# First PReLU in one ScalarE and one VectorE pass, softmax's nine exponentials in SBUF with its product on GpSimd, and new places in the order

## Chip, cores and metric

The kernel runs on one core of one Trainium2 chip. The core has five engines that run side by side, each through its own queue in order: TensorE (PE in the profile; its weight loads are PEld), VectorE (DVE), ScalarE (ACT), GpSimd (POOL) and SyncE (SP), whose queue issues all DMAs here. The metric is device time in microseconds, as the median of several runs. Before the change it is 1863.83 us, the median of 3 runs between 1862.01 and 1864.88.

## What is computed

The input x is 16 images of 256 channels by 56 by 56, fp32. Two layers follow each other, both of the form x + f(group_norm(x)). In layer 0, f takes the sign of the normalised input, convolves it three times with binarised 3 by 3 weights (dilations 1, 3, 5; 4 groups of 64 channels), passes each result through a PReLU, adds the three and normalises over channels. In layer 1, f is an attention over the 3 by 3 neighbourhood of each pixel, with 8 heads of 8 channels.

```python
# layer 0
for i, d in enumerate((1, 3, 5)):
    y = conv(sign(gn(x) + bias), binarised(w[i]), dilation=d, groups=4)
    y = y + cb[i] - move1[i]
    y = where(y >= 0, y, alpha[i] * y) + move2[i]
    out = out + y
x = x + layer_norm_over_channels(out) * gamma + beta
# layer 1
q, k_in, v_in = split(gn(x) @ qkv_w.T + qkv_b)
k, v = branch(k_in) + rpb, branch(v_in)      # 9 neighbours and a learned depthwise part
attn = softmax((q * k).sum(channels of the head), over the 9 neighbours)
x = x + (attn * v).sum(9) @ proj_w.T + proj_b
```

## The kernel before

**Tiling.** Channels lie on partitions, 64 of a group twice: the upper and the lower half of the image sit on partitions 0 to 63 and 64 to 127. An image is done in two units (u = 0, 1), each of 2 x 7 rows in both halves: 784 elements per partition. A tile in PSUM is a pair of banks ([128, 2, 512]); there are four of these pairs, and every matrix product of the kernel goes through one of them.

**Stages of an image.** `signs` reads the image, gets its group statistics (L643) and writes the signs (L667). For each unit, `conv` runs for 4 groups and 3 dilations (24 convolutions an image): 36 matmuls (L716) into a pair, then the PReLU, then `channel_norm` (L799 to L863): sums over channels by matmul (L769), mean subtraction on VectorE (L827), scaling (L837), the residual sum on GpSimd (L850), and squares for the next group norm (L854). `fold` puts the second group norm into the q/k/v weights, `qkv` makes q, k and v (L906, evicted by ScalarE at L924). `scores` multiplies q with nine shifted k (L959, the query-key products), sums them per head by matmul (L980) and does the softmax; `attend` spreads the attention by matmul (L1044), multiplies with shifted v on VectorE (L1055), adds up on GpSimd (L1070), and projects (L1087, L1097).

**The PReLU.** With z the raw product, y = csc z + cbi, and PReLU(y) = alpha y + (1 - alpha) relu(y). So each convolution takes three passes: a linear one (asc z, where asc is csc alpha), a Relu by ScalarE in place in PSUM (L750), and VectorE's scalar_tensor_tensor that adds oalpha times the Relu (L755). The linear pass is ScalarE's for the first dilation (L735, which adds the constant mv2 of the channel too) and for the third (L742, into a tile `rl`, added to `ct` later by GpSimd at L761), and VectorE's for the second (L745).

**The softmax.** Eight of the nine scores of a head lie in a transposed PSUM tile, 104 heads-by-pixels of 8 per partition (832 elements); the ninth score is zero, so that the maximum is taken against zero. The exponentials of the eight go to SBUF (`et`, L1018), that of the ninth to unused columns of the PSUM tile (L1017). Then VectorE sums eight (L1019), adds the ninth (L1021), takes the reciprocal (L1025), multiplies (L1027) and transposes back (L1031).

**What sets the order.** The program is written as a list of operations with reads and writes. `ORDER` gives each operation a place: a number for each stage and position in it, plus `PERIOD` times the image. Stages of the first image carry the sign ^, those of the last $. `Plan.emit` takes, again and again, the operation with the lowest place whose predecessors have been emitted and whose buffers are free; this is the order in each engine's queue. A very low place thus means "as soon as it can". Operations written with `either` go to GpSimd, unless `ON_VECTOR` lists their position in the stage: then VectorE does them. Buffers: four PSUM pairs, eight `ct`, one `rl`, seven `p` (products), four `m`, one each of `et` and `at`.

```python
o = Op(PERIOD * self.image + ORDER[self.stage][k], emit, bufs)
...
todo = sorted(self.ops, key=lambda o: o.place)
while todo:
    o = next((o for o in todo if not o.wait and self.room(o)), None)
```

Of the kernel before, what the change touches and what calls it, by code (L numbers as in the profile page):

```python
# [8 lines left out]
F32 = mybir.dt.float32  # L9
# [5 lines left out]
P = 128  # L15
# [57 lines left out]
class Op:  # L73
    def __init__(self, place, emit, bufs):
# [6 lines left out]
PERIOD = 1231  # L81
ORDER = {
    "conv0": (
        -682, -410, -359, -2832, -303, -327, -265, -333, -280, -264, -245, -1566, -289, -213, -969, -970,
        -319, -128, -2067, -24, -3260, -58, -18, -16, -1028, -3936, 5, 17, 18, 101, 198, -321, 208, -3768,
        197, 207, 182, -601, -3937, 20, -15, -19, -199, 30, -146, 111, -2560, 21, -394, -20, -152, -3331,
    ),
    "conv0$": (
        -685, -409, -2692, -2836, -277, -2837, -419, -253, 194, -189, 109, -866, -1791, -207, -131, -440,
        -4781, -30, -3248, 99, -154, -250, -557, -386, -2111, -2366, 32, -462, -149, -2080, 175, -1794,  # L90
        -2185, -2439, 121, 140, -6017, -1732, -220, -9, -641, 100, -155, 112, -1493, 147, -1733, 191, 240,
        149, -865, -2379,
    ),
    "conv0^": (
        -2099, -6338, -223, -5746, -1337, -3215, -66, -5779, -1241, -202, -65, -5786, -1673, 42, -67, -667,
        -358, 124, 92, 358, -3217, 123, 231, 234, -3216, 565, 167, 400, 401, -1668, 228, 318, 504, -54, 229,
        -13, 515, -1726, -288, 227, 402, -115, -71, 40, -72, 517, -1182, 702, -116, -769, -2031, 119,
    ),
    "conv1": (
        160, -122, -123, 185, 199, -740, 209, -834, 265, -287, 150, -2506, -1087, 320, 171, 170, -823, 333,  # L100
        -2428, 361, -1220, 326, -175, 180, -1339, 356, 319, 255, 254, -2493, 355, -1340, 394, -1221, 714,
        746, 632, -113, -2040, 412, -162, -296, -1322, 470, -3611, 514, -1195, 925, -1683, -2369, 905, -1995,
    ),
    "conv1$": (
        56, -644, -645, -1492, 306, -11476, -498, -11477, 418, 239, 237, -3613, 188, 148, 146, 190, -1497,
        248, -878, 152, -867, 292, 151, -2181, -2390, -2392, 192, 98, 66, -864, 773, -432, 813, -1612, 662,
        456, 455, -1613, -818, 419, -28, -29, 44, 774, -431, 816, -434, 953, 968, 284, 678, -660,
    ),
    "conv1^": (
        666, 513, 523, -1198, 726, -697, -757, 826, 776, 581, 725, 830, 871, 682, 522, 601, -2033, 828, 824,  # L110
        695, 832, 829, 724, 578, 835, 715, 711, 612, 609, -2032, 865, 831, 878, 811, 949, 902, 901, 1044,
        1106, 38, 717, 718, 827, 869, 815, 890, -2027, 922, -1136, -964, 940, 959,
    ),
    "first^": (-3247,),
    "fold": (
        1404, -2035, -892, -2087, -3779, -4755, -952, -4221, -7223, -9967, -564, -942, -953, 1414, -949,
        -562, 1455, 407,
    ),
    "fold$": (
        1238, 1089, 753, 927, 1174, 593, 772, 1298, 934, 929, 595, 268, 1484, 297, 648, 1286, 559, -6518,  # L120
    ),
    "fold^": (
        1395, -941, -2847, -582, -784, 793, 792, -861, -863, -1498, -846, 1074, 1037, 696, 1424, -847, 1481,
        1444,
    ),
    "load0": (310,),
    "load0$": (539,),
    "load0^": (744,),
    "load1": (771,),
    "load1$": (614,),  # L130
    "load1^": (-117,),
    "mean0": (
        301, -2124, -1860, -2389, 172,
    ),
    "mean0$": (
        336, 87, 139, -232, -216,
    ),
    "mean0^": (
        785, 930, 214, -4431, 979,
    ),  # L140
    "mean1": (
        719, 911, 1038, -307, 787,
    ),
    "mean1$": (
        1195, -3235, -3236, -1711, 913,
    ),
    "mean1^": (
        1117, -960, 960, -337, -336,
    ),
    "norm0": (  # L150
        -732, -3656, -2175, -2045, -918, -715, -713, -2918, -1358, -2461, -2300, -2373, -2332,
    ),
    "norm0$": (
        -967, -5586, -5587, -2008, -2009, -2388, -1206, -2970, -3775, -3776, -5599, -1156, -4352,
    ),
    "prod0": (
        -1147, 777, -1035, 1488, 156, -3123, 155, -1057, -1219,
    ),
    "prod0$": (
        963, -2462, 449, -6519, 957, -392, -6024, 421, 1095,  # L160
    ),
    "prod0^": (
        -191, 8, -2267, -2417, -1351, -1352, 444, 443, 442,
    ),
    "prod1": (
        -3102, -1021, -550, -1863, 1762, 342, 1588, -2118, 615,
    ),
    "prod1$": (
        1043, 665, 309, 1102, 1281, 244, -3472, 1119, 1163,
    ),  # L170
    "prod1^": (
        1793, 1806, 1135, -4432, 1792, -1577, -69, 348, -1895,
    ),
    "proj0": (
        2327, 2254, 2286, 373, 2370, -2325, 2451, 1869, 1844,
    ),
    "proj0$": (
        4987, -693, 3217, 1049, 3039, -1400, 2317, -1399, -580,
    ),
    "proj0^": (  # L180
        2456, 2318, 2168, 956, 2213, 403, 2375, 410, 2115,
    ),
    "proj1": (
        2596, 566, 2594, 728, 2595, 31, 2582, 972, 1998,
    ),
    "proj1$": (
        45573, -572, 3218, -571, 45772, -1396, 44708, -1395, -465,
    ),
    "proj1^": (
        2523, 2564, 2522, -2377, 2607, 2566, 2508, -689, 1823,  # L190
    ),
    "qkv0": (
        1478, 1384, 1477, 1415, 1433, 1700, 1699, 387,
    ),
    "qkv0$": (
        1002, 836, 582, 610, -2708, 1260, 689, 1285,
    ),
    "qkv0^": (
        1490, 296, 1491, 1487, 1457, 1703, 685, 732,
    ),  # L200
    "qkv1": (
        1526, 1505, 1454, 1464, 1390, 1702, 1622, 712,
    ),
    "qkv1$": (
        1016, 619, 661, -3365, -1116, 1193, -1989, 1750,
    ),
    "qkv1^": (
        1514, 1090, 1467, 206, 1432, 1716, 551, 1624,
    ),
    "root0": (  # L210
        -323, -2507, -2508, 269, 181, -248, 245, -4518, -2509, 325,
    ),
    "root0$": (
        -1114, -4877, -4950, -2612, -1167, -77, -803, -5143, -195, 480,
    ),
    "root0^": (
        675, 216, 215, -4430, 892, 917, 881, -4445, 939, 1020,
    ),
    "root1": (
        230, -453, 161, -555, 768, 847, 743, 786, 916, 1244,  # L220
    ),
    "root1$": (
        554, -859, -860, -826, 842, 1105, 841, -3528, -3551, 1178,
    ),
    "root1^": (
        618, 129, 526, -1441, 1196, 1206, 1214, -1468, -1169, 1250,
    ),
    "scale0": (
        -2391, 308, 742, -657, 311, 552, -655, 352, -518, -1336, 995, 1083,
    ),  # L230
    "scale0$": (
        -3616, -530, 790, -3617, 1003, 241, -3628, -807, 585, -793, 528, 1088,
    ),
    "scale0^": (
        810, -2704, 1097, -2294, 932, 891, 945, 931, 741, 961, 1045, 820,
    ),
    "scale1": (
        886, -1324, 1341, -426, -1325, 1353, -427, -1862, 700, -848, -1134, 721,
    ),
    "scale1$": (  # L240
        -1608, -1879, 693, -2047, 933, 1050, -258, 94, 303, 639, -285, 299,
    ),
    "scale1^": (
        814, -2794, 1299, 658, 1033, 1223, -3076, -276, 1064, -3077, 1199, 1092,
    ),
    "second^": (
        -533, -33, -269, -5855, 451, 670, -3184, -3197, -1840, -2841,
    ),
    "sign": (
        -2935, -620, -1699, -748, -537, -497, -768, -351, -1710, -526, -1611, -387,  # L250
    ),
    "sign$": (
        -1806, -587, -690, -884, -1173, -1643, -1644, -406, -940, -917, -851, -827,
    ),
    "soft0": (
        9, -22, 1683, -1162, 1642, 1681, -558, 1274, 1482, -2383, -2384,
    ),
    "soft0$": (
        -161, -12, 709, -1106, -1117, 710, 1919, 1868, 1855, 1035, 1034,
    ),  # L260
    "soft0^": (
        1489, 802, 1647, -95, 1075, 1663, -111, -1410, -1369, 1319, 1463,
    ),
    "soft1": (
        441, 1789, 2048, 1788, 2054, 2034, 798, -383, 2119, 2137, 343,
    ),
    "soft1$": (
        -1857, -1858, 882, -1233, 2421, 2422, 1504, 1503, 1507, 1506, -1172,
    ),
    "soft1^": (  # L270
        677, -14, 2019, 809, 1715, 2038, 1866, -567, 1065, 1992, 1188,
    ),
    "start^": (
        -854, -3067, -598, -1842, -4706, -3059, -2934, -2823, -589, -736, -1682, -1681, -4293, -4179, -4129,
        -3138, -588, -388, -541, -5501, -586, -532, -5502, -4128, -3068, -3064, -449, -668, -3186, -3187,
        -3169, -3168, -3181, -1702, -226, -523, -539, -5503, -481, -1363, -3182, -3183, -3105, -3754, -447,
        -225, -756, -3172, -3590, -633, -3642, -3227, -200, 288, -344, -1586, -224, -1338, -3228, -3229,
        -3211, -3212, -201, -73, -3204, -3205, -5781, -76, -85, -3206, -62, -568,
    ),
    "stats": (  # L280
        -1755, -1273, -1265, -1692, -1019, -872, -1573, -996, -832, -1698, -871, -772,
    ),
    "stats$": (
        -1727, -1368, -1559, -1883, -1776, -1654, -1805, -1349, -1361, -1807, -1215, -1183,
    ),
    "term0": (
        1553, 1554, 1552, 1536, 1566, 1565, 1629, 1621, 1610, 1609,
    ),
    "term0$": (
        1054, 1130, 1129, 1128, 1073, 1072, 1071, 996, 1028, 1027,  # L290
    ),
    "term0^": (
        1555, 1548, 1546, 1568, 1576, 1577, 1627, 1408, 1407, 1409,
    ),
    "term1": (
        1721, 1729, 1733, 1732, 1767, 1768, 1778, 1619, 1781, 1620,
    ),
    "term1$": (
        1053, 1259, 1019, 1127, 1175, 1258, 1131, 1980, 1979, 1978,
    ),  # L300
    "term1^": (
        1728, 1717, 1358, 1679, 1357, 1918, 1389, 1349, 1580, 1317,
    ),
    "value0": (
        1731, 436, 1766, 437, 1761, 1776, 434, 1760, 1775, 286, 1585, 1779, 285, -552, 2037, -373, 222, 1937,
# [45 lines left out]
}  # L351

ON_VECTOR = {
    "conv0$": (12,),
    "conv1$": (25, 51),
    "prod0": (5,),
    "prod0$": (3, 4, 6, 8),
# [1061 lines left out]
```

## Time and profile before

| | |
|---|---|
| median of 3 runs | 1863.83 us |
| the profiled execution, its own time | 1872.31 us |
| its span, first to last instruction | 1870.5 us |
| PE busy | 1653.7 us (88%) |
| DVE busy | 1570.8 us (84%) |
| POOL busy | 1408.7 us (75%) |
| ACT busy | 1314.6 us (70%) |
| DMA, mean over the span | 116 GB/s |

A line of a group names the line of the kernel, the engine, the operation, the tile written and those read, shapes, how often, then the busy time in us and the mean of one in ns, and after the second bar the idle time of the engine just before these instructions with what ended it. In windows of the trace the columns are the stretch, its length, the busy time of PE, PEld, DVE, ACT and POOL with the number of instructions in brackets, the granted clock of PE, the share of DMA time and GB/s. In the middle of the run every image shows the same pattern again.

### The profile page before, as it was taken

To read this page: it belongs to the slowest core of one execution; us is meant where nothing else is said; L and a number is where in the kernel's file an instruction comes from. 1 tells how busy PE (TensorE), PEld (TensorE's weight loads), DVE (VectorE), ACT (ScalarE), POOL (GpSimd) and SP (SyncE) were. 2 spreads that over 40 slices of the span, in tenths; PEclk is the share of its full clock that TensorE was granted. 3 is DMA by queue.
4 is the path that set the end of the run, shared out by engine and by line. 5 is a ranking of instruction groups with operands and counts; after the bars stand their busy time and mean duration, and the time that the engine had idled before them with its cause. 6 is when DMAs were issued, how large, how long until landed. Compare 5 with 4: busy or idle time off the path is not lost.

```text
span 1870.5 us, 62125 instructions
## 1 busy us (share of the span) xinstructions
PE 1653.7 (88%) x27322; PEld 953.1 (51%) x27322; DVE 1570.8 (84%) x2217; ACT 1314.6 (70%) x1861; POOL 1408.7 (75%) x782
## 2 busy tenths in 40 slices
PE   4879899898999989898998989899898989989784
PEld 3546455454545545454554545455454545745341
DVE  8777979979797997979799797979979797997966
ACT  5988778677777867677786777778677787755320
POOL 2147769688686968868696886869688686967865
PEclk9799999999999999999999999999999999999897
DMA  7852655547475554647555464755547467223023
GB/s 178 200 113 43 143 123 122 126 93 155 96 158 111 124 126 92 149 102 155 115 120 124 96 151 101 156 113 124 123 94 150 101 147 172 62 69 74 11 61 69
DMA packets 102094, 217.03 MB, mean 116 GB/s; under 512 B 10816, under 2 KB 84672, under 8 KB 101568
## 3 DMA queue, kind: packets, MB, share of 16 engines
q1 hardware_dynamic: 101824, 213.06, 51.8%
q8 instruction: 214, 3.51, 0.8%
q14 instruction: 56, 0.46, 0.1%
HBM read 156.23 MB, written 51.38 MB: 111 GB/s over the span
## 4 chain that ended last, share of the span: by engine, by line
PE 53%; POOL 18%; DVE 16%; issue 6%; ACT 4%; DMA 1%; SPq 0%; POOLq 0%; DVEq 0%; ACTq 0%
PE banks L716 19%; POOL m L1070 13%; PE banks L906 12%; PE banks L980 9%; DVE m L1055 4%; PE banks L1044 3%; PE banks L769 3%; POOL xt L850 3%; PE banks L1087 2%; ACT banks L750 2%; DVE rl L755 2%; DVE ct L755 2%; POOL p L959 1%; POOL ct L761 1%; DVE m L1075 1%
## 5 line engine op out<-in xcount | busy, mean ns | idle before, releaser
L716 PE MATMUL banks<-sgn,wconv 64*64 64x392 bf16 x13824 | 656.7, 335 | 60.3 <-DVE m L1055 25.8
L716 PEld LDWEIGHTS <-wconv 64*64 64x64 bf16 x13824 | 442.8, 106 | 279.1 <-issue 94.7
L1070 POOL TENSOR_TENSOR m<-m 128x784 f32<-128x784 f32 x255 | 475.3, 1864 | 95.9 <-DVE m L1055 82.2
L959 POOL TENSOR_TENSOR p<-qt,kt 128x784 f32<-128x784 f32 x267 | 468.1, 1789 | 93.2 <-ACT qt L924 88.0
L750 ACT ACTIVATE banks<-banks,cbi,csc 128x784 f32<-128x784 f32 x384 | 370.3, 973 | 95.8 <-DVE ct L745 95.8
L761 POOL TENSOR_TENSOR ct<-ct,rl 128x784 f32<-128x784 f32 x125 | 233.3, 1866 | 252.7 <-DVE ct L755 147.8
L1044 PE MATMUL banks<-at,wv 64*64 64x392 f32 x2560 | 276.1, 510 | 56.5 <-DVE lv L821 22.6
L1055 DVE SCALAR_TENSOR_TENSOR m<-banks,vb,vt 128x784 f32<-128x784 f32 x288 | 289.6, 1022 | 25.4 <-POOL m L1070 17.6
L755 DVE SCALAR_TENSOR_TENSOR ct<-banks,oalpha,ct 128x784 f32<-128x784 f32 x256 | 258.1, 1026 | 17.1 <-ACT banks L750 16.4
L906 PE MATMUL banks<-xt,wf 64*64 64x392 f32 x3072 | 269.0, 491 | 0.0
L850 POOL TENSOR_TENSOR xt<-xt,ct 128x784 f32<-128x784 f32 x124 | 229.2, 1871 | 1.4 <-DVE ct L837 1.3
L980 PE MATMUL banks<-p,wk 64*64 64x392 f32 x2304 | 213.7, 489 | 2.8 <-POOL p L959 2.6
L742 ACT ACTIVATE rl<-banks,asc 128x784 f32<-128x784 f32 x128 | 116.7, 912 | 107.0 <-PE banks L716 103.0
L906 PEld LDWEIGHTS banks<-xt,wf 64*64 64x64 f32 x3072 | 131.2, 133 | 101.2 <-issue 68.3
L643 ACT ACTIVATE xh<-xh 128x1568 f32<-128x1568 f32 x120 | 180.6, 1507 | 0.7
L735 ACT ACTIVATE ct<-banks,mv,asc 128x784 f32<-128x784 f32 x128 | 128.5, 1004 | 73.0 <-PE banks L716 72.8
L755 DVE SCALAR_TENSOR_TENSOR rl<-banks,oalpha,rl 128x784 f32<-128x784 f32 x128 | 131.8, 1030 | 53.6 <-ACT banks L750 48.8
L1044 PEld LDWEIGHTS banks<-at,wv 64*64 64x64 f32 x2560 | 86.8, 134 | 176.3 <-issue 69.2
L745 DVE SCALAR_TENSOR_TENSOR ct<-banks,asc,ct 128x784 f32<-128x784 f32 x128 | 131.0, 1024 | 24.9 <-PE banks L716 21.3
L980 PEld LDWEIGHTS banks<-p,wk 64*64 64x64 f32 x2304 | 93.1, 133 | 93.4 <-issue 76.2
L854 ACT ACTIVATE ct<-xt,pr 128x784 f32<-128x784 f32 x128 | 120.2, 940 | 25.4 <-POOL xt L850 23.0
L1087 PE MATMUL banks<-m,wp 64*64 64x392 f32 x1024 | 106.4, 518 | 32.1 <-DVE m L1075 29.6
(115 smaller groups left out, 1870.6 us busy)
## 6 DMA issues: line engine op xcount, KB each, us to landing
xh<-in_x SPq DMA_DIRECT2D x248, 392.0 KB, 5.7
xt<-in_x SPq DMA_DIRECT2D x128, 392.0 KB, 9.2
out<-xt SPq DMA_DIRECT2D x128, 392.0 KB, 5.9
sgn<-sgn SPq DMA_DIRECT2D x128, 41.2 KB, 7.6
p<-in_w SPq DMA_DIRECT2D x12, 144.0 KB, 3.2
xt<-in_wk_parts SPq DMA_DIRECT2D x1, 1344.0 KB, 8.1
xt<-in_wv_parts SPq DMA_DIRECT2D x1, 1280.0 KB, 9.4
wq<-in_wqkv SPq DMA_DIRECT2D x1, 384.0 KB, 9.7
```

Of the source, the lines that this page charges most:

```text
L643: lambda func=func, col=col: nc.scalar.activation(inside(g) if b == 0 else image(xh), image(xh), func, accum_out=sums[:, col : col + 1]),
L716: nc.tensor.matmul(out=ps[q * GC : (q + 1) * GC, h, 0:SN], lhsT=wconv[h * GC : (h + 1) * GC, g, d, tap, :], rhs=sgn[g][h * GC : (h + 1) * ...
L750: lambda: nc.scalar.activation(n(), n(), AF.Relu, bias=cbi[:, g, s], scale=csc[:, g, s]),
L755: lambda: nc.vector.scalar_tensor_tensor(to.tile, n(), oalpha[:, g, s], to.tile, ALU.mult, ALU.add),
L761: lambda e: e.tensor_tensor(ct.tile, ct.tile, to.tile, ALU.add),
L850: lambda e, g=g: e.tensor_tensor(xt[:, g], xt[:, g], ct[g].tile, ALU.add),
L906: nc.tensor.matmul(out=ps[h * D : (h + 1) * D, q, 0:SN], lhsT=wf[q * GC : (q + 1) * GC, g, j, :], rhs=xt[q * GC : (q + 1) * GC, g, h, :], ...
L959: e.tensor_tensor(p.tile.rearrange("p x (r w) -> p x r w", w=W), _view(qt[:, 0, u * SN :], [(NU * SN + LANES, 2), (W, SR), (1, W)]), shift ...
L980: nc.tensor.matmul(out=ps[q * D : (q + 1) * D, h, 0:n], lhsT=wk[r, j, :], rhs=rhs, start=s == 0, stop=s == 9,)
L1044: nc.tensor.matmul(out=ps[h * D : (h + 1) * D, q, 0:SN], lhsT=wv[q * D : (q + 1) * D, j, :], rhs=at[q * D : (q + 1) * D, h, 0:SN], start=True,
L1055: lambda j=j, m=m, ps=ps: nc.vector.scalar_tensor_tensor(m.tile.rearrange("p x (r w) -> p x r w", w=W), _view(ps[:, 0, :], [(512, 2), (W, ...
L1070: lambda e, m=m, acc=acc: e.tensor_tensor(acc.tile, acc.tile, m.tile, ALU.add),
```

## The change

Four things change.

First dilation: ScalarE's Identity pass is dropped. ScalarE's Relu reads PSUM and writes `ct` in SBUF, with its scale and bias already multiplied by |1 - alpha|; VectorE then adds the linear part to it in the one pass that it had. Where 1 - alpha is negative, the whole sum is carried with its sign turned (`sg0`), which the channel mean (`cms` in place of `cm32`), the mean subtraction (now scalar_tensor_tensor) and mv2 take into account. The constant mv2 moves to the third dilation's linear pass, which becomes an Identity with a bias.

Softmax: the nine exponentials of a head lie side by side in a new SBUF tile `e9` (`ex`, rows of 9). The sum runs over nine, the small addition goes, the reciprocal is taken in SBUF, and the product with it is written with `either`: GpSimd, or VectorE where `ON_VECTOR` says so.

Setup: some small VectorE instructions more.

Places: `PERIOD` goes from 1231 to 1201, all of `ORDER` is new, and `ON_VECTOR` too. For the 14 middle images, products 2 and 5 of unit 0 and product 6 of unit 1 are now VectorE's (before: product 5 of unit 0 alone), and so is unit 0's softmax product. Over the run VectorE has 53 query-key products (before 21), 16 of the 32 softmax products, and of the other sums three (before eight).

```diff
-PERIOD = 1231
+PERIOD = 1201
...
 ON_VECTOR = {
-    "conv0$": (12,),
-    "conv1$": (25, 51),
-    "prod0": (5,),
-    "prod0$": (3, 4, 6, 8),
-    "prod0^": (3,),
-    "prod1$": (1, 6),
+    "conv0$": (35,),
+    "prod0": (2, 5),
+    "prod0$": (3, 5, 6),
+    "prod0^": (1, 4),
+    "prod1": (6,),
+    "prod1$": (0, 1, 4, 5),
+    "prod1^": (0, 1),
     "scale0$": (7,),
-    "scale0^": (10,),
-    "scale1$": (4,),
-    "scale1^": (4,),
-    "value0^": (4,),
+    "scale1$": (7,),
+    "soft0": (8,),
+    "soft0^": (8,),
+    "soft1$": (8,),
 }
...
-        if d == 0:
+        stt = nc.vector.scalar_tensor_tensor
+        if d in POOLED:
             act(
                 lambda: nc.scalar.activation(
-                    ct.tile, n(), AF.Identity, bias=mv2[:, g : g + 1], scale=asc[:, g, s]
+                    to.tile, n(), AF.Identity, bias=mv2[:, g : g + 1], scale=asc[:, g, s]
                 ),
...
         act(
-            lambda: nc.scalar.activation(n(), n(), AF.Relu, bias=cbi[:, g, s], scale=csc[:, g, s]),
-            [("scales", g, d)],
-            [ps],
+            lambda: nc.scalar.activation(
+                n() if d else ct.tile, n(), AF.Relu, bias=cbi[:, g, s], scale=rsc[:, g, s]
+            ),
+            [("scales", g, d)] if d else [ps, ("scales", g, d)],
+            [ps] if d else [ct],
         )
...
+        if d:
+            dve(lambda: stt(to.tile, n(), oalpha[:, g, s], to.tile, ALU.mult, ALU.add), [ps], [to])
+        else:
+            dve(
+                lambda: stt(ct.tile, n(), asc[:, g, s], ct.tile, ALU.mult, ALU.add),
+                [ps, ("scales", g, d)],
+                [ct],
+            )
...
-                lambda g=g: nc.vector.tensor_tensor(ct[g].tile, ct[g].tile, mb[:, :, 0:SN], ALU.subtract),
+                lambda g=g: stt(
+                    ct[g].tile, ct[g].tile, sg0[:, g : g + 1], mb[:, :, 0:SN], ALU.mult, ALU.subtract
+                ),
...
-        act(lambda: nc.scalar.activation(ninth(), each(e8.tile), AF.Exp, scale=-1.0), [e8], [(tp, "ninth")])
-        act(lambda: nc.scalar.activation(et.tile, tv(), AF.Exp, scale=-1.0), [tp], [et])
-        dve(lambda: nc.vector.tensor_reduce(each(sm.tile), lanes(et.tile), AX.X, ALU.add), [et], [sm])
-        dve(
-            lambda: nc.vector.tensor_tensor(ninth(), each(sm.tile), ninth(), ALU.add),
-            [sm],
-            [(tp, "ninth")],
+        act(lambda: nc.scalar.activation(ex[:, :, CH], e8.tile, AF.Exp, scale=-1.0), [e8], [(ex, 1)])
+        act(
+            lambda: nc.scalar.activation(
+                ex[:, :, 0:CH].rearrange("p (b n) t -> p b n t", b=2), lanes(tv()), AF.Exp, scale=-1.0
+            ),
+            [tp],
+            [(ex, 0)],
         )
-        dve(lambda: nc.vector.reciprocal(ninth(), ninth()), [], [(tp, "ninth")])
-        dve(
-            lambda: nc.vector.tensor_tensor(lanes(et.tile), lanes(et.tile), wide(ninth()), ALU.mult),
-            [(tp, "ninth")],
+        dve(lambda: nc.vector.tensor_reduce(sm.tile, ex.tile, AX.X, ALU.add), [(ex, 0), (ex, 1)], [sm])
+        dve(lambda: nc.vector.reciprocal(sm.tile, sm.tile), [], [sm])
+        either(
+            lambda e: e.tensor_tensor(
+                et.tile.rearrange("p b (n t) -> p (b n) t", t=CH),
+                ex[:, :, 0:CH],
+                sm.tile.unsqueeze(2).broadcast_to([P, NBK, CH]),
+                ALU.mult,
+            ),
+            [sm, (ex, 0)],
             [et],
         )
```

## The prediction, made before the result was known

> **What bounds the kernel now.** I began with the head of the page, then cut one middle image into stretches, asked there what TensorE (PE) waited for, and last looked up single rows. The page's first part:
>
> ```profile
> PE 1653.7 (88%) x27322; PEld 953.1 (51%) x27322; DVE 1570.8 (84%) x2217; ACT 1314.6 (70%) x1861; POOL 1408.7 (75%) x782
> ```
>
> No engine is full, but an average hides stages. The chain in order of time shows the same long stretch of q/k/v products (L906) at 155.60 us in image 0 and at 1688.01 in image 14, 14 spacings on: 109.46 us each. One image, from one fold to the next, cut where PE begins to wait (columns: length, then busy time of PE, PEld, DVE, ACT, POOL, granted clock, DMA share, GB/s):
>
> ```profile
> 474.90:535.50 60.60, 59.87 (x1015) 34.37 (x1014) 45.84 (x73) 48.69 (x73) 47.06 (x27) 1.00 0.52 114
> 535.50:580.40 44.90, 37.27 (x624) 20.60 (x624) 44.17 (x57) 31.35 (x42) 38.63 (x22) 1.00 0.68 145
> 580.40:584.10 3.70, 3.70 (x64) 2.55 (x60) 3.70 (x4) 1.98 (x4) 2.50 (x2) 1.00 0.02 4
> ```
>
> In the first 60.6 us PE has no gap: whatever is taken off DVE, ACT or POOL there is hidden, and DVE has 14.8 us to spare. In the next 44.9 us DVE is full (44.17) and PE idles 7.6. Over the image PE works 100.84, DVE 93.71, POOL 88.20, ACT 82.02. The waits of PE between 256 and 1567 us (12 images; us in total, times, longest):
>
> ```profile
> PE banks L716 <- DVE m L1055: 24.4, 24, 1.1
> PE banks L1087 <- DVE m L1075: 19.7, 12, 2.0
> PE banks L1044 <- DVE lv L821: 19.3, 12, 2.0
> PE banks L716 <- DVE ct L837: 13.5, 12, 1.1
> PE banks L1044 <- DVE rl L755: 9.3, 12, 0.8
> ```
>
> All are DVE: PE waits until DVE has emptied a PSUM pair, or has made the operand. No wait on ACT is among the large ones. So the kernel is PE-bound for 60% of an image and DVE-bound for 40%. What can be won is at most PE's idle time, 109.46 - 100.84 = 8.6 us an image.
>
> **The change, part by part.** Rows that price it:
>
> ```profile
> L750 ACT ACTIVATE banks<-banks,cbi,csc 128x784 f32<-128x784 f32 x384 | 370.3, 973 | 95.8 <-DVE ct L745 95.8
> L742 ACT ACTIVATE rl<-banks,asc 128x784 f32<-128x784 f32 x128 | 116.7, 912 | 107.0 <-PE banks L716 103.0
> L735 ACT ACTIVATE ct<-banks,mv,asc 128x784 f32<-128x784 f32 x128 | 128.5, 1004 | 73.0 <-PE banks L716 72.8
> L827 DVE TENSOR_TENSOR ct<-ct,banks 128x784 f32<-128x784 f32 x128 | 117.7, 961 | 0.2 <-PE banks L783 0.2
> L1019 DVE TENSOR_REDUCE mx<-et 128x104 f32<-128x832 f32 x32 | 32.6, 1018 | 0.6 <-ACT et L1018 0.6
> L1027 DVE TENSOR_TENSOR et<-et,banks 128x832 f32<-128x832 f32 x32 | 32.4, 1014 | 0.6
> L1021 DVE TENSOR_TENSOR banks<-mx,banks 128x104 f32<-128x104 f32 x32 | 8.5, 266 | 1.6
> 490.02 0.97 DVE L959 TENSOR_TENSOR p<-qt,kt 128x784 f32<-128x784 f32 x1 [6.15 <-ACT qt L924]
> 1794.00 5.79 DVE L959 TENSOR_TENSOR p<-qt,kt 128x784 f32<-128x784 f32 x3 [8.78 <-ACT qt L924]
> ```
>
> *First PReLU.* Eight convolutions an image lose the Identity pass (8 x 1.004). Their Relu now goes from PSUM to SBUF: I price it as L735, which has that route and the same two per-partition operands, 1004 against 973, +0.03 x 8. The third dilation's pass gains a bias: L742 becomes L735, +0.092 x 8. ACT: -8.03 + 0.25 + 0.74 = -7.0 an image, 82 to 75. The DVE pass on it stays one pass of 1.02. ACT is not on the path in either stretch, so at its own value this is zero; what it does is free each of those PSUM pairs a pass (1.0 us) earlier.
>
> *Mean subtraction* becomes scalar_tensor_tensor: 1.02 (as L837) for 0.96, 8 x 0.06 = +0.5 of DVE.
>
> *Softmax, twice an image.* The sum runs over 936 elements instead of 832: 1.018 x 936/832 = 1.145, +0.13. The small add goes, -0.27. Reciprocal and sum now read SBUF. [...] The wide exponential writes rows of 8 at a pitch of 9: between nothing and +0.1, on ACT, hidden. The product: for unit 1 of middle images it leaves DVE (-1.01) for POOL; for unit 0 it stays on DVE. On POOL nothing like it ran. By L959's 1.789 for 784 elements it is 832 x 2.28 ns = 1.9 us. [...] The PSUM pair is released after the exponential and not after the product: in this image 3.3 us earlier for unit 0 (516.8 for 520.1) and 5.7 for unit 1. With the eight convolutions that is about 17 of 4 x 109 us of pair time.
>
> *More query-key products on DVE.* The table of exceptions puts products 2 and 5 of unit 0 and product 6 of unit 1 on DVE, one before: -3.6 on POOL, two more on DVE. The last two fenced lines price them. Alone, or started together with POOL's, one takes 0.97. Three in a row beside POOL's products took 5.79: the second and third each waited for the running POOL instruction (2.4 to 2.5 each), while a POOL product hit by one takes 2.5 instead of 1.73. An instruction of two SBUF operands and a POOL instruction thus exclude each other. Softmax's product, when it stays on DVE, becomes such an instruction too, since its divisor moves from PSUM to SBUF. Bounds: two more at 0.97 to 2.49, the softmax product +0 to +1.5. I take 2.49 for the neighbour of product 5 (they lie side by side in the table), 1.7 for unit 1's, +0.8 for softmax. Behind product 2 on DVE's queue wait the PSUM evictions; but in this image DVE stood idle for 3.08 us right after its one product (491 to 494), while PE had work, so that is the cover. If it is gone, PE waits up to 1.5.
>
> *Sum for DVE*: +4.2 products, +0.8 - 1.0 softmax products, +0.25 - 0.53 sum and add, +0.5 mean: +4.2, at best +1.2. DVE goes to 95 to 98 an image, PE stays at 100.8, POOL -3.6 + 1.9 and up to +2.4 of stretching: 86.5 to 89.
>
> *On the path.* DVE's additions lie mostly in the first stretch (products from 490 to 528, unit 0's softmax at 512 to 521), where it has 14.8 us spare. In the DVE-bound stretch lie unit 1's softmax (531 to 548) and four mean subtractions: -1.01 - 0.27 + 0.13 + 0.25 = -0.9 us an image. That is what the edits give if nothing else moves.
>
> *New places.* Every instruction's rank is new, so this part cannot be read from the trace, only bounded: 0 to -8.6. One number helps: the image distance in places, 1231 before for 109.46 us. Places track time roughly (the first fold at 1404 and the last projection at 2596 lie 104 us apart in the trace, 11.4 places per us, and 1231 / 109.46 = 11.2). At that rate 1201 means 106.8, -2.7. What is late then is again DVE's emptying of PSUM. I take -2.3, the 2.7 less 0.4 for exclusion that the table may not count.
>
> *Head and tail.* From 38 to 147 us ACT is the fullest (96.8 of 109); image 0's eight passes go: between 0 and -7, taken -4. The setup gains some ten small DVE instructions at about 0.16: +1.5 at most, beside weight loading. In the last 194 us PE works 150; unknown, -10 to +10, taken 0.
>
> *Total*: 14 x -2.3 - 4 = -36 us. The profiled execution took 1872.31 (span 1870.5): 1836. The median of the runs is 8.5 lower, 1863.83: **1828 us**.
>
> **Rivals.** *Slower: exclusion.* Unit 1's product on DVE and unit 0's softmax product fall where DVE is full and POOL busy, at their worst prices: 2.49 and 1.5 more than before, 4.0 together, less the 0.9 that leaves: +3.1 an image, 14 x 3.1 - 4 = +39, 1903. It decides once more than about 1.2 us of DVE time an image (the 0.9, and 4/14 from the head) moves into a full stretch. For it: the exclusion is plain in the tail, and POOL is 86% busy in the second stretch. Against it: the spare 14.8 us of the first. *Nothing:* ACT was never on the path, the new order trades one wait for another; only the head gains, about 1860. For it: no PE wait on ACT; against it: DVE loses 0.9 in the stretch where it sets the pace. *More:* the new order spreads DVE evenly and PE never stops for long, 103.5 an image: 14 x -6 - 4 = -88, 1776. Against it: DVE would be 93% busy with only four PSUM pairs between it and PE.
>
> **Chances.** As forecast (1800 to 1850) 0.54; more (below 1800) 0.12; nothing (1850 to 1872) 0.12; slower by exclusion (above 1872) 0.22. Range 1790 to 1890: it leaves out about 0.09 below and 0.10 above. A measurement here can tell 0.2%, 3.7 us. Faster by over that: 0.54 + 0.12 + half of nothing, 0.72; within 0.05; slower 0.23.
>
> **What would show it.** Image spacing near 107 us, with PE's idle near 6 per image; ACT 1733 instructions or so (128 fewer), about 1205 us busy; POOL 771 instructions; DVE products averaging 1.7 us. Exclusion shows as DVE products and softmax products at 2.4 us in the full stretch and a spacing over 109.5. I am wrong if the spacing falls though DVE's sum grows beyond 98, or if PE comes to wait on POOL's softmax product.

## The result, and the profile after

The changed kernel takes 2002.08 us (median of 4 runs, 1989.55 to 2020.27) against 1862.92 for the one before (1861.89 to 1864.88): a ratio of 1.072, 95% interval 1.065 to 1.080. It is slower by 7%, where 1828 us and a gain had been forecast. The ratio and its interval leave out the longest run, 2020.27 us, which counts as slow. The profiled execution took 1989.55 us (span 1987.3).

The first part of the page after, and three of its groups:

```profile
PE 1684.7 (85%) x27322; PEld 947.0 (48%) x27322; DVE 1727.6 (87%) x2206; ACT 1211.7 (61%) x1733; POOL 1412.7 (71%) x771
```

```profile
L972 DVE TENSOR_TENSOR p<-qt,kt 128x784 f32<-128x784 f32 x53 | 204.8, 3895 | 42.2 <-ACT qt L937 39.5
L743 ACT ACTIVATE rl<-banks,mv,asc 128x784 f32<-128x784 f32 x128 | 128.2, 1002 | 106.4 <-PE banks L723 104.2
L1042 POOL TENSOR_TENSOR et<-e,mx 128x832 f32<-128x832 f32 x16 | 26.2, 1639 | 6.3 <-DVE mx L1040 6.0
```

ACT did what was expected (1733 instructions, 103 us less), POOL too (771 instructions). The one row out of line is the first: VectorE's query-key products, 53 of them, average 3.895 us. A mean of that size over an operation of 0.97 us hides two kinds. Single instructions show them. The timeline of DVE and then of POOL in image 2 (columns: start in us, length in us, then the instruction; POOL's rows fold up to five instructions into one):

```profile
411.23 1.02 DVE L1017 TENSOR_REDUCE mx<-banks 128x104 f32<-128x832 f32 x1
412.28 1.03 DVE L1020 SCALAR_TENSOR_TENSOR banks<-mx,banks 128x832 f32<-128x832 f32 x1
413.22 15.51 DVE L972 TENSOR_TENSOR p<-qt,kt 128x784 f32<-128x784 f32 x1
428.65 1.12 DVE L1039 TENSOR_REDUCE mx<-e 128x104 f32<-128x936 f32 x1
```

```profile
412.62 5.10 POOL L972 TENSOR_TENSOR p<-qt,kt 128x784 f32<-128x784 f32 x3
417.65 1.87 POOL L772 TENSOR_TENSOR ct<-ct,rl 128x784 f32<-128x784 f32 x1
419.47 8.43 POOL L972 TENSOR_TENSOR p<-qt,kt 128x784 f32<-128x784 f32 x5
```

VectorE's product 6 of unit 1 takes 15.51 us. It begins at 413.22, when POOL has been at work without a break for 23.0 us, and ends at 428.73, 0.8 us after POOL's last instruction of that run (419.47 + 8.43 = 427.90). VectorE did not wait for the one POOL instruction in its way, as the products in the trace before had done (2.49 us at most), but for nine in a row, until POOL had nothing left to do. I call such an instruction held. Eight of the 14 middle images have one, of 15.47 to 15.51 us; in five others the same product took 1.88 to 1.94, and in image 14, where it comes 18.2 us into a run, 1.75. Two rows of image 4, one of the five:

```profile
656.05 1.88 DVE L972 TENSOR_TENSOR p<-qt,kt 128x784 f32<-128x784 f32 x1
659.84 2.23 DVE L1042 TENSOR_TENSOR et<-e,mx 128x832 f32<-128x832 f32 x1
```

Here the product comes 23.0 us into POOL's run as well, and unit 0's softmax product 26.8 us into it; neither is held.

What it costs is seen by setting an image with a held product beside the next one without (windows from fold to fold; columns as in the section on the profile before), and what PE waited for in the two:

```profile
506.70:628.50 121.80, 103.87 (x1696) 57.88 (x1693) 110.16 (x130) 75.46 (x108) 87.20 (x48) 0.94 0.50 110
628.50:738.40 109.90, 102.41 (x1694) 57.62 (x1690) 97.83 (x130) 75.40 (x108) 88.65 (x48) 0.98 0.55 122
```

```profile
PE banks L1064 <- DVE g L612: 11.7, 1, 11.7
PE banks L723 <- DVE ct L838: 2.5, 2, 2.0
```

The two rows of waits are the first image's; the first of them is missing from the second's list. Behind the held product stand, in DVE's queue, softmax's sum and, further back, a small statistics step (L612), and PE stops for 11.7 us until that step is done. The window is 11.9 us longer.

Fold to fold, the middle images are 118.04 us apart on average, against 109.38 before: eight with a held product average 122.1, the other five 111.6. Thirteen spacings at +8.66 are 112.6 us; the first spacing gives +4.0, the last +1.9, the tail +5.6, the head -7.1: 117 in all, which is the difference of the spans (1987.3 - 1870.5). Why one of the five without a held product (738 to 854 us) is 115.6 long is not shown.

### The profile page after: what moved, and what is told of

Its sections match the earlier page's. It is cut to its first block, busy times and chain, and to the rows that moved or that the text cites. A ratio compares the mean times of both kernels' runs of the same rounds, so it can differ in the third digit from the quotient of the medians.

```text
span 1987.3 us, 61837 instructions
## 1 busy us (share of the span) xinstructions
PE 1684.7 (85%) x27322; PEld 947.0 (48%) x27322; DVE 1727.6 (87%) x2206; ACT 1211.7 (61%) x1733; POOL 1412.7 (71%) x771
## 4 chain that ended last, share of the span: by engine, by line
PE 35%; DVE 30%; ACT 13%; DMA 7%; issue 7%; POOL 5%; SPq 2%; POOLq 0%; ACTq 0%; DVEq 0%
PE banks L723 13%; DVE p L972 8%; PE banks L919 8%; PE banks L993 5%; DVE ct L838 4%; PE banks L1064 4%; DVE m L1075 4%; ACT banks L756 3%; DVE xt L1117 3%; POOL p L972 3%; DMA sgn<-sgn 3%; PE banks L1107 2%; DMA xh<-in_x 2%; ACT rl L743 2%; ACT ct L867 2%
## 5 line engine op out<-in xcount | busy, mean ns | idle before, releaser
L723 PE MATMUL banks<-sgn,wconv 64*64 64x392 bf16 x13824 | 673.7, 339 | 64.4 <-DVE ct L838 34.3
L772 POOL TENSOR_TENSOR ct<-ct,rl 128x784 f32<-128x784 f32 x127 | 241.8, 1904 | 324.4 <-DVE rl L763 139.8
L972 POOL TENSOR_TENSOR p<-qt,kt 128x784 f32<-128x784 f32 x235 | 430.9, 1869 | 27.4 <-ACT qt L937 27.4
L756 ACT ACTIVATE banks<-banks,cbi,rsc 128x784 f32<-128x784 f32 x256 | 247.5, 973 | 48.8 <-DVE ct L751 48.5
L972 DVE TENSOR_TENSOR p<-qt,kt 128x784 f32<-128x784 f32 x53 | 204.8, 3895 | 42.2 <-ACT qt L937 39.5
L756 ACT ACTIVATE ct<-banks,cbi,rsc 128x784 f32<-128x784 f32 x128 | 126.5, 1001 | 121.9 <-PE banks L723 121.6
L743 ACT ACTIVATE rl<-banks,mv,asc 128x784 f32<-128x784 f32 x128 | 128.2, 1002 | 106.4 <-PE banks L723 104.2
L993 PEld LDWEIGHTS banks<-p,wk 64*64 64x64 f32 x2304 | 85.0, 132 | 127.8 <-issue 72.5
L751 DVE SCALAR_TENSOR_TENSOR ct<-banks,asc,ct 128x784 f32<-128x784 f32 x128 | 130.2, 1025 | 11.9 <-PE banks L723 11.3
L763 DVE SCALAR_TENSOR_TENSOR ct<-banks,oalpha,ct 128x784 f32<-128x784 f32 x128 | 130.0, 1026 | 11.5 <-ACT banks L756 11.4
L766 DVE SCALAR_TENSOR_TENSOR ct<-banks,asc,ct 128x784 f32<-128x784 f32 x128 | 130.1, 1026 | 7.3 <-ACT ct L756 7.0
```

What stands on the lines that cost most here:

```text
L723: nc.tensor.matmul(out=ps[q * GC : (q + 1) * GC, h, 0:SN], lhsT=wconv[h * GC : (h + 1) * GC, g, d, tap, :], rhs=sgn[g][h * GC : (h + 1) * ...
L756: lambda: nc.scalar.activation(n() if d else ct.tile, n(), AF.Relu, bias=cbi[:, g, s], scale=rsc[:, g, s]),
L763: dve(lambda: stt(to.tile, n(), oalpha[:, g, s], to.tile, ALU.mult, ALU.add), [ps], [to])
L772: lambda e: e.tensor_tensor(ct.tile, ct.tile, to.tile, ALU.add),
L972: e.tensor_tensor(p.tile.rearrange("p x (r w) -> p x r w", w=W), _view(qt[:, 0, u * SN :], [(NU * SN + LANES, 2), (W, SR), (1, W)]), shift ...
L993: nc.tensor.matmul(out=ps[q * D : (q + 1) * D, h, 0:n], lhsT=wk[r, j, :], rhs=rhs, start=s == 0, stop=s == 9,)
```

## The experiments

Theory from here on: the loss is VectorE held off by GpSimd when it reads two operands from SBUF, and the edits are priced nearly right. Rivals: the new places are slow in themselves; the held instruction only shows a lateness that has another cause. Each ratio is against runs of the kernel before that were made alongside, with medians between 1862.56 and 1868.84.

**The held product given back to GpSimd.** From the changed kernel:

```diff
-    "prod1": (6,),
```

> The changed kernel with one entry less: product 6 of unit 1 in the middle images goes back from VectorE to GpSimd. Theory (that one VectorE product is shut out by GpSimd's run of products, 15.5 us in 9 of 14 images): every image spacing falls to the 110 us of the five images that escaped, so 9 x 12 us go, about 1880 us (1865 to 1895). Rival (the new order as a whole, or the other edits, cost the time): 1960 us or more.

Measured: 2021.31 us, ratio 1.082 (1.075 to 1.088). A miss: it lies in the rival's range. (Eight images had a long product, not nine.) The hold did not go, it moved to the next VectorE instruction with two SBUF operands, unit 0's softmax product, in 13 of the 14 middle images:

```profile
L1041 DVE TENSOR_TENSOR et<-e,mx 128x832 f32<-128x832 f32 x16 | 178.6, 11164 | 0.6
```

It came 26.9 us into POOL's run and took 13.3 each time. Images were 121.2 us apart.

**The same product put on VectorE in the kernel before.**

```diff
+    "prod1": (6,),
```

> The kernel before with one entry more: product 6 of unit 1 in the middle images on VectorE, nothing else changed. Theory (shutting out is a matter of two operands in SBUF beside a full GpSimd queue, not of the new order): the product takes 2 us where it gets in behind one GpSimd instruction and 15 us or so where it does not; with all images shut out up to 1863 + 14 x 12 = 2030 us, with none 1863 to 1890. Rival (specific to the new order): no such instruction over 2.6 us, 1863 to 1875.

Measured: 1868.53 us, ratio 0.9999 (0.9983 to 1.0016). It took 1.3 to 1.65 us in twelve middle images, where it arrives at the last POOL instruction of a run, and 2.41 and 0.96 in the last two. DVE's extra 1.4 us an image cost nothing. That is the rival's outcome and also the theory's lowest case, so this run alone doesn't part the two; it shows that the operation is not dear in itself.

**The PReLU part alone**, in the kernel before, at its places without those of the dropped pass; core of the edit:

```diff
-        if d == 0:
+        if d in POOLED:
...
-            lambda: nc.scalar.activation(n(), n(), AF.Relu, bias=cbi[:, g, s], scale=csc[:, g, s]),
+            lambda: nc.scalar.activation(
+                n() if d else ct.tile, n(), AF.Relu, bias=cbi[:, g, s], scale=rsc[:, g, s]
+            ),
```

> The kernel before with the first-PReLU part alone (Identity pass dropped, its place in the order dropped with it, the rest of the order unchanged). As predicted: ACT 7 us less an image and off the path, the mean subtraction 0.5 us more of VectorE; between 1850 and 1866 us. Rival (earlier release of PSUM pairs is what TensorE waits for): below 1845. Rival (the slower mean subtraction lies in the VectorE-bound stretch and decides): above 1868.

Measured: 1885.2 us, ratio 1.009 (1.006 to 1.012). In the middle images ACT does 6 us less, and the spacing stays at 109.1 to 109.3: the part gains nothing there. The total is above the forecast, in the range of the rival with the slower mean subtraction, but not for its reason, since the middle images are no longer. One instruction was held again, the residual addition that the last image puts on VectorE, after 33.3 us of POOL at work:

```profile
1732.20 6.57 DVE L677 TENSOR_TENSOR xt<-xt,ct 128x784 f32<-128x784 f32 x1
```

The last two image distances are 115.7 and 103.0 against 112.2 and 97.0: +9.5 of the 11.0 us that the spans differ by. The hold lies in the first of the two; that all of the 9.5 comes from it is not shown.

**Both to GpSimd**, in the changed kernel: neither unit 1's product nor unit 0's softmax product stays on VectorE.

```diff
-    "prod1": (6,),
-    "soft0": (8,),
```

> The changed kernel with two entries less: product 6 of unit 1 and the softmax product of unit 0 both go to GpSimd in the middle images, so VectorE keeps products 2 and 5 of unit 0, which start with GpSimd's run. Theory (any VectorE instruction with two SBUF operands that arrives in the middle of a GpSimd run is shut out until the run ends): none arrives there now, no such instruction over 2.6 us, spacing 109 to 111 us, 1865 to 1895 us. Rival (the new order costs the time by itself): 1950 us or more, with spacing over 117 though no VectorE instruction is long.

Measured: 1995.96 us, ratio 1.071 (1.069 to 1.073). No VectorE instruction is long any more, and it is as slow as before, with images 118.4 us apart. That is what the rival had said, and not the 1865 to 1895 us expected. The waits of DVE between 260 and 1570 us:

```profile
DVE at L1049 <- POOL et L1040: 118.5, 11, 10.8
```

Unit 0's softmax product now stands in POOL's queue behind up to six others, most of them products of unit 1, and DVE's queue waits at the transpose behind it for 10.8 us an image. The hold has become a wait in the queue, 10.8 us where the holds took 13.3 and 15.5: both are set by POOL's run. So this run does not yet tell the new places from the hold; the one with the divisor in PSUM, below, does.

**Both, and product 2 too**, as before the change:

```diff
-    "prod0": (2, 5),
+    "prod0": (5,),
```

> As the kernel with both of them on GpSimd, and product 2 of unit 0 on GpSimd as well, so that VectorE has one two-operand product an image, as before the change. Theory: 2.5 us less of VectorE an image, in the stretch where it has time to spare; between the other kernel's time and 14 us below it, 1855 to 1890. Rival (VectorE is what ends last there too): 25 us or more below.

Measured: 2012.72 us, ratio 1.080 (1.078 to 1.082): also a miss (1855 to 1890 us expected). More work on POOL makes it worse, though DVE falls to 91.6 us an image.

**The softmax part alone, product on GpSimd**, in the kernel before:

```diff
-        tp, et, at = Buf("ps"), Buf("et"), Buf("at")
+        tp, ex, et, at = Buf("ps"), Buf("e9"), Buf("et"), Buf("at")
...
+        dve(lambda: nc.vector.reciprocal(sm.tile, sm.tile), [], [sm])
+        either(
```

> The kernel before with the softmax part alone and its product always on GpSimd, the order otherwise unchanged (the place of the dropped addition goes). As predicted: VectorE loses 1.0 + 0.27 - 0.13 us a softmax, partly in the stretch where it sets the pace; 1850 to 1866. Rival (the product waits in GpSimd's queue behind up to several instructions of 1.8 us, and the matmuls that need the attention wait with it): above 1880.

Measured: 1928.37 us, ratio 1.035 (1.034 to 1.037); images 113.0 apart. The rival came true. DVE gives up 2.5 us an image (93.7 to 91.2) and waits for POOL's product instead (28.8 us in 12 images at the transpose).

**The softmax part alone, product on VectorE**, divisor in SBUF; to the last edit comes, for both units and all images:

```diff
+    "soft0": (8,),
...
+    "soft1": (8,),
...
```

> The kernel before, at its own places, with the softmax part of the change (nine exponentials in SBUF, one sum, the divisor in SBUF) but the normalising product on VectorE for both units in all images. Theory (the price is the shut-out, and at these places it comes when a product arrives deep in a GpSimd run): unit 0's product arrives in the midst of GpSimd's run as it did before the change, so it is either 1.0 to 2.6 us (then images 109 to 111 us apart, 1860 to 1885 us) or, if the age is a bad one, 10 us and more in most images (116 to 121 us apart, 1960 to 2030 us). Rival (two SBUF operands cost nothing at these places, and two fewer small instructions save time): no product above 1.1 us, 109 us apart, 1850 to 1863 us.

Measured: 1986.52 us, ratio 1.065 (1.062 to 1.068). At the old places, with the old PReLU, unit 0's product arrives 29.4 us into POOL's run and is held 8.3 us in twelve middle images, 7.7 and 6.6 us in the last two; images 118.1 apart. The row over both units:

```profile
L853 DVE TENSOR_TENSOR et<-e,mx 128x832 f32<-128x832 f32 x32 | 136.1, 4252 | 0.6
```

So the new places are not needed for the loss.

**The divisor in PSUM.** The changed kernel with unit 1's product on GpSimd and the reciprocal of unit 0 written to unused columns of the score's PSUM tile, as before the change:

```diff
-    "prod1": (6,),
...
-        dve(lambda: nc.vector.reciprocal(sm.tile, sm.tile), [], [sm])
+        dve(lambda: nc.vector.reciprocal(divisor(), each(sm.tile)), [sm], [k])
...
-                sm.tile.unsqueeze(2).broadcast_to([P, NBK, CH]),
+                over(divisor()),
...
```

> The changed kernel with its softmax product kept on VectorE where it was, but with the reciprocal written to PSUM, so that this product reads one operand from SBUF and one from PSUM; and with the ninth query-key product of unit 1 given to GpSimd. Nothing on VectorE between images then reads two SBUF operands except query-key products 2 and 5 of unit 0, which were never held for more than 2.5 us. Theory (the loss is VectorE standing shut out while GpSimd runs, and in GpSimd's queue where the product was moved there): no VectorE tensor_tensor above 2.6 us, unit 0's softmax product at 1.0 to 1.1 us in every image, images about 110 us apart, 1865 to 1890 us. Rival (the new places themselves are late, and the long waits are only where the lateness shows): images still 116 us or more apart with no long VectorE instruction, 1950 to 2010 us.

Measured: 1876.77 us, ratio 1.0057 (1.003 to 1.008), as the theory expected. The product's row, and one image:

```profile
L1052 DVE TENSOR_TENSOR et<-e,banks 128x832 f32<-128x832 f32 x16 | 16.3, 1020 | 0.6
```

```profile
505.00:614.50 109.50, 102.45 (x1698) 56.94 (x1690) 95.00 (x130) 75.53 (x108) 88.70 (x50) 0.98 0.55 123
```

VectorE, ScalarE and GpSimd do the same instructions in the same order here as in the run with unit 1's product on GpSimd (the first experiment). The same softmax product at the same place, with one operand moved from SBUF to PSUM, falls from 13.3 us to 1.02, and the kernel from 2021 to 1877. Images are 109.43 us apart, as before the change (109.38).

**When is an instruction held?** Four runs do none of the reference's computation, only bursts of GpSimd products beside which VectorE issues one instruction with two SBUF operands at a chosen moment; one sweeps the moment in the changed kernel itself, by a delay ahead of the product. The age of the meeting is how long the GpSimd instruction that VectorE meets has been running. The core of a burst in the last run (the others differ in length, 10, 12 or 26 products, and in the passes over PSUM, whose sizes stand here as `passes`), and of the delay:

```python
for i in range(CHAIN):
    nc.gpsimd.tensor_tensor(rows(pp[i % BUFS]), rows(go), shifted(i % 9), ALU.mult)
...
for k in passes:
    nc.vector.scalar_tensor_tensor(
        p2[:, :, 0 : k // 2], ps[:, :, 0 : k // 2], go[:, 0, 0:1], kt[:, :, 0 : k // 2], ALU.mult, ALU.mult
    )
nc.vector.tensor_tensor(rows(pd), rows(go), shifted(4), ALU.mult)
...
for n in (*[40] * (12 * b // 40), 12 * b % 40):
    if n:
        nc.vector.reciprocal(pad[:, 0:n], pad[:, 0:n])
```

> No part of the computation is done: 33 times, ten GpSimd products of 784 elements stand ready in a row, and one VectorE product with both operands in SBUF is started at a moment that moves by 0.05 us from burst to burst (it follows on a VectorE instruction on PSUM of 32 to 1568 elements). Theory: two outcomes, a wait for the running GpSimd instruction (up to 2.6 us) or for all of the ten (up to 17 us), and which of them hangs on the phase. Rival (GpSimd gives way after each instruction): no VectorE product over 2.6 us.

> No part of the computation is done: 75 bursts of twelve GpSimd products standing ready; the VectorE instruction with two SBUF operands comes 5 to 7 us after the run's start, its moment moving by 0.067 us from burst to burst, in three series: whole tiles; the shifted views that the query-key products read; whole views on GpSimd and the softmax product's operands (rows of 8 at a pitch of 9, and a divisor repeated 8 times) on VectorE. Theory (arriving in the middle of a run is what shuts it out): instructions of 8 us or more in every series. Rival 1 (the access pattern decides): in the last two series alone. Rival 2 (neither): none over 2.6 us.

> The changed kernel with a chain of small reciprocals on a scratch tile ahead of unit 1's VectorE product in images 1 to 14: 12 elements more with each image, so that the product meets GpSimd's instruction at an age that grows by about 0.08 us from image to image, from about 0.7 us upwards. Theory (which age the product meets decides whether it is let through at the end of that instruction or only at the end of GpSimd's run): some images with 1 to 2.6 us and some with 10 us and more, in contiguous bands of age. Rival A (the place deep in a long run decides, whatever the age): 10 us and more in all images. Rival B (only the narrow band seen, 0.58 to 0.646 us, is bad): none above 2.6 us in images with an age above 0.66. The output is the reference's; the time is not used.

> None of the reference's computation: 138 bursts of 26 GpSimd products; in each, VectorE meets GpSimd with two products at the start, then works 19 to 21 us from PSUM, then issues one instruction with two SBUF operands (110 times a query-key product, 28 times a softmax product), each burst 14 elements later than the one before, so that a whole GpSimd instruction is stepped through in about 15 ns steps. Theory (a run over 20 us old and the age together make the shut-out): in one or two bands of age the VectorE instruction takes 15 us and more, to the end of the run, elsewhere 1.0 to 2.6. Rival (it takes something else that the kernel does at the same time): always 1.0 to 2.6 us.

> None of the reference's computation: 208 bursts of 26 GpSimd products; in each, VectorE issues one query-key product with two SBUF operands after 3, 6, 9, 12, 15, 18, 21 or 24 passes over PSUM (arrivals spread over about 3 to 26 us into GpSimd's run), at 13 ages each, once with and once without two VectorE products at the start of the run. Theory (the longer GpSimd has run without a break, the likelier it is that a VectorE instruction is held to the run's end): none of 13 held at the shallow depths, about half at 24, growing between; with an early meeting or without makes no difference. Rival A (the early meetings bring it about): held only in the series that has them. Rival B (it depends on how many GpSimd instructions are still queued): held most at the shallow depths.

With 10 or 12 products in a burst (33 and 75 bursts, arrivals up to some 7 us into the run) nothing was held: 0.97 to 2.6 us, always the rest of the running POOL instruction, whatever its age. That is the price of my prediction, and it would have held there. In the changed kernel with the moment shifted from image to image, 10 of 14 products were held and 4 not, at ages that mix: held at 0.06, 0.60, 0.75, 0.90, 1.16 and 1.60 us among others, let through at 0.82, 1.32 and 1.67 (and at 0.98 in image 14, only 20.0 us into a run). So the theory that the age alone decides fell, and with it both rivals. With 26 products in a burst and an arrival 23.9 to 25.7 us into the run, 70 of 138 were held, each for 20 to 22 us, and none took between 2.5 and 20. Ages and forms of the instruction mix again, with no clean bands of age as expected; the share grows with the depth, from 20 of the 68 that met the 14th GpSimd product of the run to 50 of the 70 that met the 15th. The last run, 208 bursts, sweeps the depth. Of all arrivals up to 24.5 us none was held. Without an earlier meeting all seven from 26.8 us on were held, and none before. With one earlier meeting (one product was issued ahead, not two) eight of 13 from 24.7 us on were held, the others let through. This is against rival B, since the shallow arrivals met more GpSimd instructions still queued. From one of the first kind, DVE and then POOL:

```profile
4411.33 5.33 DVE L56 SCALAR_TENSOR_TENSOR p<-banks,go,kt 128x784 f32<-128x784 f32 x5
4416.57 17.55 DVE L59 TENSOR_TENSOR pd<-go,big 128x784 f32<-128x784 f32 x1
```

```profile
4389.82 43.47 POOL L52 TENSOR_TENSOR pp<-go,big 128x784 f32<-128x784 f32 x26 [0.97 <-ACT go L50]
```

It arrives 26.8 us into the run and ends 0.8 us after POOL's 43.47 us are over. The passes ahead of it, which read PSUM and one SBUF operand, go on at 1.04 us beside the same run. Without an earlier meeting it is a step and not the slow growth that I expected, and an earlier meeting shifts it: there both my theory and its first rival were half right.

**The sum of nine without the hold**, at the old places: nine exponentials in SBUF, reciprocal in PSUM, product on VectorE for both units.

```diff
-        dve(lambda: nc.vector.reciprocal(sm.tile, sm.tile), [], [sm])
-        either(
-            lambda e: e.tensor_tensor(
+        dve(lambda: nc.vector.reciprocal(divisor(), each(sm.tile)), [sm], [(tp, "ninth")])
+        dve(
+            lambda: nc.vector.tensor_tensor(
```

> The kernel before, at its own places, with the nine exponentials side by side in SBUF and one sum over them, but with the reciprocal written to PSUM and the product on VectorE for both units, so that no added instruction reads two SBUF operands. Theory (the shut-out is the whole loss of the softmax part; the sum over nine saves an addition of some 0.27 us per unit on VectorE, which does not bound the image by itself): no VectorE tensor_tensor above 2.6 us, images 109 to 109.5 us apart, 1855 to 1868 us. Rival (the small exponential into SBUF and the later freeing of the exponentials cost as well): 110 us apart or more, 1870 to 1890 us.

The diff is against the changed kernel's softmax. Measured: 1862.3 us, ratio 0.9991 (0.9982 to 1.0000), images 109.45 apart, as expected. It is the best that I found of the change, and no gain that a measurement here can tell.

## Why the prediction was wrong

*The bound on the exclusion* is the step that failed: "two more at 0.97 to 2.49, the softmax product +0 to +1.5". I read from the trace before that a VectorE instruction waits for the one POOL instruction that is running, and took this as the worst price. The products of the trace before agreed (up to 2.5 us), but none came later than 16.9 us into a POOL run. Deep in a run the price can be the rest of the run: 15.5 us, 13.3, 8.3, 6.6 in four kernels. A bound of one POOL instruction was no bound.

The trace before has a row that speaks against the bound, in the setup; DVE, then POOL:

```profile
3.78 6.94 DVE L1118 TENSOR_SCALAR oalpha<-pr 128x12 f32<-128x12 f32 x1
```

```profile
0.73 8.56 POOL L537 MEMSET sgn<- 128x2508 bf16 x4 [0.29 <-POOLq L1406]
9.23 1.46 POOL L537 MEMSET qt<- 128x1632 f32 x1
```

This VectorE instruction on 12 elements starts 3.1 us into POOL's run and ends at 10.72, after the fourth memset that it met (9.23 + 1.46 = 10.69). In the kernel before with one more product on VectorE, whose setup is the same, it took 1.29 us, to the end of the first. It has one operand and POOL only writes there, so it may be another case than the held products; but it shows that one POOL instruction is not the longest wait.

*The rival "slower: exclusion"* had the mechanism and the side (1903), with the same wrong price: 3.1 us an image where 8.7 were measured. Its place was right: unit 1's product and unit 0's softmax product.

*New places*, -2.3 us an image from the ratio of the two `PERIOD`s: wrong as well. With the hold taken away (divisor in PSUM, unit 1's product on GpSimd) the spacing is 109.43 at PERIOD 1201 against 109.38 at 1231. So the distance in places did not tell the time, and what is left over the kernel before (1876.8 to 1865.3) lies in the ends: in the profiled executions the head is 4.0 shorter, the first two spacings are 6.1 longer and the tail 4.2.

*ACT -7.0 an image, worth nothing on the path*: right. In the changed kernel ACT falls by 6.8 an image, and the PReLU part alone leaves the middle spacing where it was. That freeing PSUM pairs earlier would help, on which the -2.3 leaned, no run shows.

*The rows*: L1042 on POOL took 1.64 us where I took 1.9. The third dilation's pass took 1.002 (predicted 1.004), the Relu to SBUF 1.001, the mean subtraction 1.023, the sum over nine 1.117 (1.145), the reciprocal 0.798 after 0.811, a difference near zero. The small exponential took 0.395 instead of 0.262, hidden.

*DVE's sum*, 95 to 98: 97.8 in an image without a hold, 110.2 with one.

*Head -4, tail 0*: -7.1 and +5.6 in the profiled execution. The -7.1 is not all gain: the trace before has the long wait in the setup shown above, and the kernel before with one more product, without that wait, reaches its first fold 5.3 us earlier than the trace before.

*What would show it*: I had named products and softmax products at 2.4 us in the full stretch and a spacing over 109.5. The spacing said it; the products were at 15.5, or in its place 13.3.

What stays open is the cause of the hold. The overlap of POOL's records does not tell it: in the long sweep (138 bursts) the last two POOL records ahead of an arrival overlap by 47.8 ns on average where it was held and by 42.2 where it was not, but single values mix (32 to 69 and 31 to 57), and in the last sweep there is no such difference (41.5 and 40.7 among arrivals from 24.7 us on). So no run shows why one arrival is held and another let through.

One thing goes with being let through. Outside the setup, no instruction with two SBUF operands was held in any trace that came less than 17.8 us after VectorE's last such instruction in the same run. Fourteen of these came 23 us and more into the run, and all got through: the softmax product of image 4 above, 1.9 us after unit 1's, is one, and image 0's, 30.9 us into a run and 7.0 after another, is too. That a turn for VectorE starts the count again would fit these numbers; it is my guess, and no run varied this alone. Nor is a long run without a turn enough: with the softmax part alone and its product on VectorE, image 0's came 28.8 us into a run as the first and took 2.1. Breaking POOL's run by a wait, in the kernel, was not tried.

## What to carry to other kernels

Before an operation is put on VectorE with both operands in SBUF, look how long GpSimd has been working without a break when it arrives: after some 23 us the price may be the rest of GpSimd's run, and not one instruction (here 6.6 to 22 us where it was held). The longest wait seen in a trace of one order bounds nothing for another order (2.5 us for a product before the change, 15.5 after). Keep one operand of such an operation in PSUM where it costs nothing (here the divisor: 1.02 us against 13.3), or let it arrive at the end of a run (1.3 to 1.65 us in the kernel before). An operation with a queue behind it is no better moved to GpSimd if it then stands behind the same run (with both products there, 10.8 us of waiting an image and a ratio of 1.071, against 1.072 for the changed kernel).

## What the runs showed of the hardware

- A VectorE instruction with two SBUF operands can be kept waiting while GpSimd works on, and the records show it as one instruction of that length: 15.5 us in the changed kernel, 20 to 22 us in 70 of the 138 bursts of the long sweep.
- The earliest hold of a product in any trace was 23.0 us into a GpSimd run. All 283 meetings in the first, the second and the last sweep that came less than 23.4 us into a run cost no more than the running instruction (2.6 us at most).
- A GpSimd query-key product that yields to one takes 2.44 to 2.51 us instead of 1.72 (the bursts of 26).
- In the two images shown, TensorE's granted clock is 0.94 with the hold and 0.98 without, and its busy time for the same work 103.9 against 102.4 us. Over the middle images it is 0.93 to 0.96 in the eight with a hold and 0.94 to 1.00 in the five others.
